# Silu tiles laid out group by group, and the stores of the first two gates moved to the end of pairs 4 and 5

## The chip, the core and the metric

The kernel runs on one core of one Trainium2 chip. The metric is the device time of one execution in microseconds (us). The kernel before took 1743.54 us (median of 3 runs, 1742.93 to 1745.15); the one execution that was profiled took 1740.37 us, of which the span from its first to its last instruction is 1738.6 us.

## What is computed

The input x has 4 images of 128 channels and 96 x 96 pixels. Each image is group-normalised and read as a sequence of 9216 steps in four orders (by rows and by columns, each forward and reversed). Each sequence goes through the same block:

```python
t = _grouped1x1(x, in_proj_w, in_proj_b, G)
u, gate = (t[:, :HID], t[:, HID:])
u = jax.nn.silu(u)
u = lax.conv_general_dilated(u, dw_w, ..., feature_group_count=HID)   # 5 taps per channel
s = _conv1x1(u, ssm_in_w)
a = DMIN + (DMAX - DMIN) * jax.nn.sigmoid(_conv1x1(u, ssm_delta_w, ssm_delta_b))
bb, cc = tanh of two more 1x1 products of u
hst = linear recurrence along the sequence: h = a * h + bb * s
u = u + _conv1x1(cc * hst + ssm_d[None, :, None] * s, ssm_out_w)
u = _grouped1x1(u * jax.nn.sigmoid(gate), mix_w, mix_b, G)
y = _conv1x1(u, out_proj_w, out_proj_b)
```

The four outputs are put back in image order, multiplied by the fuse matrix, summed, and added to x. All of it is float32; there are 256 hidden channels (`HID`) and 32 state channels (`MH`).

## The kernel before

**Tiling.** Two sequences that run in opposite directions are worked on side by side (index `s`). A sequence is cut into 6 strips of 16 lines (`NS`), a strip into 4 interleaved phases (`R`) of 384 columns (`N`). A *step* is one strip of the two sequences; a *pair* is one phase of a step for both of them, and the main loop runs over 192 pairs: `pair(t)` for t = 0 to 5, then `pair_on(t)`, which also finishes pair t - 6. Eight passes (4 images, two orientations) have 24 pairs each (`NP`).

**The silu tile.** `front` computes, 4 pairs ahead of their use, the silu of one of the 4 groups `g` of a step: TensorE multiplies `x_in` by the normalised input weights (L130, called from `in_proj_tile`) and ScalarE applies silu (L514) into `sils[step]`. That tile holds 2 sequences `s`, 2 halves of the channels `j`, 4 groups `g` and 385 columns, indexed `[:, s, j, g, :]`. It is read by the convolution's matmuls (`conv`, `conv_less`), by the taps on ScalarE and VectorE (`taps`, L729 and L731), and by DMAs.

**What is kept in DRAM.** The second half of a pass uses the silu of the first half's strips again, mirrored: the third and second strip's from SBUF, the first strip's from DRAM. So the silu of the first strip of each pass is stored group by group (`keep_silu`, L494) and loaded back for the last strip (`load_silu`, L500): 64 such DMAs in the kernel. Likewise the tanh of the gates of the first 12 pairs of a pass are stored to `kept` and loaded later. In the first pass the gate of pair n is worked out in two halves, in pairs 2n and 2n + 1 (L580), n = 0, 1, 2; gates 0 and 1 stay in the two SBUF tiles `gates[0]`, `gates[1]` until pairs 6 and 7 use them, gate 2 goes into a shared tile and is loaded back from DRAM at pair 6 (L599). The stores are issued at the end of pairs 1, 3 and 5 (L935). The silu stores of the first pass are issued at the end of pairs 0 and 1.

**Order of the work.** The order is written out by hand. Every DMA but one is issued by SyncE (SP), in program order. A DMA names one of eight semaphores in turn, so that one of them also waits until the DMA eight places ahead of it has landed. The work around the change is that of pairs 0 to 7. There, `pair(t)` does on TensorE: convolution of the pair, `front(t + 4)`, projections of the pair (`u,main` in the rows), the gate's product. The rows of `x_in` for the next step are loaded by `after_front` (L297): half of them one phase at a time, after each group, and the other half for all four phases at once after group 3, which for step 2 is in pair 3. Pair 4 computes `front(8)`, the first group of step 2, and needs those. `load_gate` (L315) loads rows for gates, `load_chunks` (L429) chunks of the next image for its statistics, `keep_lone` (L663) stores and `load_lone` (L669) loads two edge rows of a step's silu.

Of the kernel before, what the change touches and what calls it, by code (L numbers as in the profile page):

```python
# [42 lines left out]
F32 = mybir.dt.float32  # L43
# [4 lines left out]
P = 128  # L48
# [11 lines left out]
N = LN * WW // R  # L60
# [8 lines left out]
def conv_preact_kernel(  # L69
# [9 lines left out]
    nc = tc.nc  # L79
# [221 lines left out]
    def gate_at(un):  # L301
        return (un["p"] + PAD) % R, (un["p"] + PAD) // R

    def mirror(n):

        if n % NP < NP // 2:
            return None
        st, k = divmod(n % NP, R)
        return (NS - 1 - st) * R + TURN.index(R - 1 - TURN[k])

    def load_gate(i):
        if i < NU and mirror(i // 2) is None:
            un = units[i]
            q, _ = gate_at(un)
            nc.sync.dma_start(  # L315
                x_in[un["s"]][half(1 - un["s"]), q, :],
                xs[un["b"], un["lay"], half(1 - un["s"]), q, bass.ds(un["st"] * N, N + 1)],
            )
# [63 lines left out]
    for s in range(2):  # L382
# [18 lines left out]
    wk = ctx.enter_context(tc.tile_pool(name="work", bufs=2))  # L401

    gates = [wk.tile([P, 2, 2, N], F32, tag=f"gate{e}", bufs=1, name=f"gate{e}") for e in range(2)]
    kept = [
        [dp.tile([P, 2, 2, N], F32, tag=f"kept{e}_{m}", name=f"kept{e}_{m}") for m in range(NP // 2)]
        for e in range(2)
    ]
# [25 lines left out]
    def stats_chunks(t):  # L433
# [5 lines left out]

    sils = {}  # L440

    kept_sil = [
        [dp.tile([P, 2, 2, N + 1], F32, tag=f"sil{e}_{g}", name=f"sil{e}_{g}") for g in range(R)]
        for e in range(2)
# [6 lines left out]
    def front_parts(i, banks, half=False):  # L451

        step, g = divmod(i, R)
        if step * UB >= NU:
            return
        st = step % NS
        if st in (NS // 2, NS // 2 + 1):
            sils[step] = sils[step - 1 - 2 * (st - NS // 2)]
        elif st == NS - 1 and g < 3:
            load_silu(step, (g + 1,))  # L460
        elif g == 0 and fresh(step):
            sils[step] = wk.tile([P, 2, 2, 4, N + 1], F32, tag="sil", name=f"sil_{step}")
        if fresh(step):
            yield from compute_front(step, g, banks, half)
        if st == 0:
            for j in range(2):
                edges(step, g, j, nc.gpsimd)
        after_front(step, g)
# [26 lines left out]

    def load_silu(step, gs):
        if 0 in gs:
            sils[step] = wk.tile([P, 2, 2, 4, N + 1], F32, tag="sil", name=f"sil_{step}")
        for g in gs:
            nc.sync.dma_start(sils[step][:, :, :, g, :], kept_sil[step // NS % 2][g])  # L500

# [86 lines left out]
    def keep(n):  # L588
        return kept[n // NP % 2][n % NP]
# [3 lines left out]
    def tile_of(n):  # L593
        return gates[n % 2]
# [8 lines left out]
    def load_last(t):  # L603

        n = NU // 2 - R
        if t == n:
            lasts.append(wk.tile([P, 2, 2, 4, N + 1], F32, tag="sil", name="last_gates"))
        for e in ((0, 1), (), (2,), (3,))[t - n]:
            old_gates[n + e] = lasts[0][:, :, :, e, :N]
            nc.sync.dma_start(old_gates[n + e], kept[n // NP % 2][mirror(n + e)])  # L610

    lasts = []
# [285 lines left out]
    early = [None]  # L898

    def pair(t):  # L900
        i = 2 * t
        banks = head_banks(t)
        if t == R:
            load_lone(1)
        if t:
            new_u(i)
            taps(i, range(1, K))
            single = alone(units[i]["p"])
            conv(i, banks, single)
            if single:  # L910
                add_lone(i, banks)
            else:
                conv_less(i, banks, False)
                for s in range(2):
                    nc.vector.tensor_copy(us[i][:, s, 0, :], bank(min(banks) + s)[:, :N])
            first_tap(i + 2)
            front(t + R, FRONT if banks == PROJ else (5, 4, 2, 3))
        recurrence(t)
        stats_chunks(t)
        load_chunks(t + 2)  # L920
        proj(i, banks)
        n, s = divmod(t, 2)
        if s == 0:
            early[0] = tile_of(n) if n < 2 else shared()[:, : 4 * N].rearrange(
                "p (s j n) -> p s j n", s=2, j=2
            )
        for j in range(2):
            gate(2 * n, s, j, 2 + j)
        for j in range(2):
            tanh_one(n, early[0], s, j, 2 + j)  # L930
        load_gate(2 * n + s + UB)
        for g in {0: (0, 1), 1: (2, 3)}.get(t, ()):
            keep_silu(0, g)
        if s:
            nc.sync.dma_start(kept[0][n], early[0])  # L935
        if t > 0:
            s = tbs[i - 2][0:64, :]
            nc.gpsimd.tensor_scalar(s, s, d_sb[0:64, 0:1], None, ALU.mult)
# [232 lines left out]
    def start():  # L1171
        def filler(n):
            nc.tensor.matmul(
                bank(7)[:, :n], accf[:, bass.ds(10 * SC, P)], accf[:, bass.ds(10 * SC, n)],
                start=True, stop=True,
            )

        def outer(d, i, copy):
            for j in range(2):
                nc.tensor.matmul(  # L1180
                    bank(i)[:, bass.ts(j, P)], w_out[:, bass.ts(j, P)], w_fuse[:, d, :],
                    start=True, stop=True,
                )
            copy(w_of[:, d].rearrange("p j c -> p (j c)"), bank(i)[:, : 2 * P])

        def inner(ds, i):
            for n, (d, j) in enumerate((d, j) for d in ds for j in range(2)):
                nc.tensor.matmul(  # L1188
                    bank(i)[:, bass.ts(n, P)], w_mix[:, j, :], w_of[:, d, j, :],
                    start=n == 0, stop=True, skip_group_check=True,  # L1190
                )
            to = w_fin[:, ds[0] : ds[-1] + 1].rearrange("p d j c -> p (d j c)")
            nc.vector.tensor_scalar_mul(to, bank(i), 0.5)

        pieces = stats_first(b0)
        for n in (512, 512, 512):
            filler(n)
        next(pieces)
        for n in (512, 512):
            filler(n)  # L1200
        next(pieces)
        outer(0, 0, nc.scalar.copy)
        outer(1, 1, nc.scalar.copy)
        next(pieces)
        outer(2, 4, nc.scalar.copy)
        next(pieces)
        outer(3, 5, nc.vector.tensor_copy)
        filler(128)
        for _ in pieces:
            pass  # L1210
        sils[0] = wk.tile([P, 2, 2, 4, N + 1], F32, tag="sil", name="sil_0")
        banks = ((2, 3), (6, 7), (0, 1), (4, 5)), ((2, 3), (6, 7), (4, 5), (2, 3))

        def burst(j, g):
            for s in range(2):
                in_proj(0, g, s, j, banks[j][TURN.index(g) if j else g][s])

        def silus(j, g):
            for s in range(2):
                silu(0, g, s, j, banks[j][TURN.index(g) if j else g][s])  # L1220
            edges(0, g, j, nc.vector)

        def load_rows(j, r):
            for s in range(2):
                load_front(1, s, slice(64 * s + 32 * j, 64 * s + 32 * j + 32), r)

        for g in range(R):
            burst(0, g)
        silus(0, 0)
        burst(1, TURN[0])  # L1230
        silus(0, 1)
        burst(1, TURN[1])
        silus(0, 2)
        inner((0, 1), 0)
        inner((2, 3), 1)
        for w in (w_of, w_fuse):
            for e in (2, 1):
                nc.gpsimd.tensor_add(w[:, 0:e], w[:, 0:e], w[:, e : 2 * e])
        load_rows(0, slice(0, R))
        load_rows(1, slice(TURN[0], TURN[0] + 1))  # L1240
        silus(0, 3)
        new_u(0)
        burst(1, TURN[2])
        silus(1, TURN[0])
        taps(0, (0,), nc.vector)
        burst(1, TURN[3])
        load_rows(1, slice(TURN[1], R))
        load_rows(1, slice(0, TURN[0]))
        silus(1, TURN[1])
        taps(0, (1,))  # L1250
        conv(0, head_banks(0))
        silus(1, TURN[2])
        taps(0, (2,))
        silus(1, TURN[3])
        conv_less(0, head_banks(0))
        taps(0, (3, 4))
        keep_lone(0)
        load_lone(0)
        pf = bank(3)
        terms = [(w_of[:, 0, j, :], b_mix[:, j : j + 1]) for j in range(2)] + [(w_fuse[:, 0, :], b_out)]  # L1260
        for i, (lhsT, rhs) in enumerate(terms):
            nc.tensor.matmul(pf[:, 0:1], lhsT, rhs, start=(i == 0), stop=(i == len(terms) - 1))
        nc.scalar.activation(b_fin, pf[:, 0:1], AF.Identity, bias=b_fuse)
# [94 lines left out]
```

## Time and profile before

| | us |
|---|---|
| median of 3 runs | 1743.54 (1742.93 to 1745.15) |
| profiled execution, whole | 1740.37 |
| its span, first to last instruction | 1738.6 |
| TensorE busy | 1715.3 |
| VectorE busy | 1504.6 |
| ScalarE busy | 1494.7 |
| GpSimd busy | 1452.5 |
| DMA packets | 176,436 with 363.47 MB, a mean of 209 GB/s |

In the rows of the profile PE is TensorE's matmul, PEld its weight load, DVE VectorE, ACT ScalarE, POOL GpSimd and SPq the queue of SyncE that issues DMAs. L130 is line 130 of the kernel. A row of a timeline gives start, duration, engine, line, operation, `out<-in`, shape, a count, and in square brackets how long the engine was idle ahead of it and what ended that. A row that merges several instructions runs from the first one's start to the last one's end. A row of DMAs gives the size of one and the median time from issue to landing. The granted TensorE clock is 1.00 throughout.

### The profile page before, as it was taken

What the parts mean: (1) busy time and instruction counts of PE and PEld (TensorE: products, weight loads), DVE (VectorE), ACT (ScalarE), POOL (GpSimd) and SP (SyncE); (2) the same over time, 40 slices, a digit from 0 to 9 for tenths busy, and PEclk for the clock granted to TensorE, in tenths of its full rate; (3) what the DMA queues carried; (4) which work ended last, traced back from release to release, by engine and by line L of the source; (5) the groups of instructions that cost most, each with busy time, mean ns of one, the idle gap of its engine ahead of it and who ended that gap; (6) DMA issues with size and microseconds to landing.
All of it is one profiled execution on the core that took longest, in us unless ns stands there. A gap on an engine that the chain in (4) does not pass through costs nothing.

```text
span 1738.6 us, 54363 instructions
## 1 busy us (share of the span) xinstructions
PE 1715.3 (99%) x22626; PEld 644.7 (37%) x22626; DVE 1504.6 (87%) x1505; ACT 1494.7 (86%) x2544; POOL 1452.5 (84%) x1496
## 2 busy tenths in 40 slices
PE   7999999999999999999999999999999999999998
PEld 3233333333333433344333443334333343333333
DVE  6899998888889999888888999888888888888897
ACT  4788888889888898888988888888998888888875
POOL 3589889888779988988788988898878889887887
PEclk9999999999999999999999999999999999999999
DMA  7846965368984786337896488433897549743465
GB/s 239 229 157 202 300 194 151 116 214 271 283 280 151 249 272 200 116 124 255 257 309 226 151 298 258 145 120 133 290 287 249 179 140 294 213 135 135 148 224 167
DMA packets 176436, 363.47 MB, mean 209 GB/s; under 512 B 16704, under 2 KB 150848, under 8 KB 176192
## 3 DMA queue, kind: packets, MB, share of 16 engines
q1 hardware_dynamic: 176048, 359.96, 64.7%
q8 instruction: 179, 2.93, 0.7%
q14 instruction: 65, 0.53, 0.1%
q10 hardware_dynamic: 144, 0.04, 0.0%
HBM read 221.41 MB, written 138.53 MB: 207 GB/s over the span
## 4 chain that ended last, share of the span: by engine, by line
PE 95%; DMA 2%; DVE 1%; ACT 1%; issue 0%; SPq 0%; DVEq 0%
PE psum L130 81%; PE psum L564 8%; PE psum L544 5%; DMA x_in<-in_xs 1%; DVE psum L731 1%; DMA acc<-in_xr 0%; DVE u L625 0%; ACT psum L576 0%; DVE u L731 0%; ACT psum L729 0%; SPq L327 0%; PE psum L1188 0%; ACT sil L514 0%; ACT t L777 0%; ACT shared L580 0%
## 5 line engine op out<-in xcount | busy, mean ns | idle before, releaser
L731 DVE SCALAR_TENSOR_TENSOR psum<-sil,small,psum 128x768 f32<-128x768 f32 x576 | 589.1, 1023 | 42.1 <-ACT psum L729 16.6
L130 PE MATMUL psum<-u,w_fin 128*32 128x384 f32 (+1 forms) x6192 | 541.6, 484 | 1.1 <-ACT ys L847 0.5
L130 PE MATMUL psum<-u,main 128*32 128x384 f32 x6144 | 535.1, 489 | 0.5 <-DVE u L678 0.4
L625 DVE SCALAR_TENSOR_TENSOR u<-gate,psum 128x768 f32<-128x768 f32 x376 | 341.8, 950 | 154.7 <-PE psum L564 54.5
L866 POOL TENSOR_TENSOR acc<-ys,acc 128x384 f32<-128x384 f32 x375 | 422.7, 1149 | 13.9 <-ACT ys L847 1.9
L812 POOL TENSOR_TENSOR t<-t,t 64x384 f32<-64x384 f32 (+1 forms) x192 | 277.4, 1445 | 70.8 <-DVE t L806 53.6
L576 ACT COPY psum<-u 128x768 f32<-128x768 f32 x384 | 301.4, 799 | 10.5 <-DVE u L625 4.4
L130 PEld LDWEIGHTS psum<-u,w_fin 128*32 128x32 f32 x6192 | 195.9, 110 | 308.8 <-issue 235.7
L130 PEld LDWEIGHTS psum<-u,main 128*32 128x32 f32 x6144 | 180.0, 109 | 324.5 <-issue 217.4
L130 PE MATMUL psum<-sil,band 128*32 128x384 f32 x3072 | 285.3, 488 | 0.0
L779 POOL TENSOR_SCALAR t<-tm 64x384 f32<-64x384 f32 x184 | 172.5, 937 | 113.4 <-ACT tm L768 101.5
L813 POOL TENSOR_TENSOR t<-t,t 64x384 f32<-64x384 f32 (+1 forms) x192 | 233.9, 1218 | 15.1
L780 POOL TENSOR_TENSOR t<-t,tm 64x384 f32<-64x384 f32 x192 | 213.1, 1110 | 28.4 <-ACT t L771 13.6
L564 PE MATMUL psum<-t,main 32*128 32x384 f32 x1536 | 228.3, 525 | 4.2 <-ACT psum L576 4.2
L729 ACT ACTIVATE psum<-sil,small 128x768 f32<-128x768 f32 x191 | 172.4, 903 | 62.0 <-DVE u L625 60.1
L731 DVE SCALAR_TENSOR_TENSOR u<-sil,small,psum 128x768 f32<-128x768 f32 x192 | 194.9, 1015 | 6.8
L514 ACT ACTIVATE sil<-psum,bnorm 128x385 f32<-128x385 f32 x384 | 191.8, 584 | 7.4 <-PE psum L130 5.2
L544 PE MATMUL psum<-x_in,wn 32*128 32x384 f32 x768 | 161.6, 498 | 0.0
L849 ACT COPY ys<-psum 128x384 f32<-128x384 f32 x288 | 132.4, 478 | 32.9 <-PE psum L130 27.3
L130 PEld LDWEIGHTS psum<-sil,band 128*32 128x32 f32 x3072 | 88.9, 108 | 171.4 <-issue 63.3
L768 ACT ACTIVATE tm<-psum,small 128x384 f32<-128x384 f32 x192 | 110.8, 577 | 16.3 <-PE psum L130 6.2
L564 PEld LDWEIGHTS psum<-t,main 32*128 32x128 f32 x1536 | 94.0, 183 | 73.7 <-issue 42.9
(106 smaller groups left out, 1510.9 us busy)
## 6 DMA issues: line engine op xcount, KB each, us to landing
gate<-kept SPq DMA_DIRECT2D x114, 768.0 KB, 5.7
kept<-gate SPq DMA_DIRECT2D x74, 768.0 KB, 3.6
sil<-sil SPq DMA_DIRECT2D x64, 770.0 KB, 7.8
lone<-edge SPq DMA_DIRECT2D x40, 770.0 KB, 8.5
x_in<-in_xs SPq DMA_DIRECT2D x250, 96.2 KB, 3.3
edge<-sil SPq DMA_DIRECT2D x96, 192.5 KB, 3.9
out<-acc SPq DMA_DIRECT2D x46, 384.0 KB, 6.9
acc<-in_xr SPq DMA_DIRECT2D x39, 384.0 KB, 6.7
```

Of the source, the lines that this page charges most:

```text
L130: nc.tensor.matmul(o[r, : rhs.shape[-1]], lhsT, rhs, start=start, stop=stop, skip_group_check=True)
L514: nc.scalar.activation(sils[step][:, s, j, g, :], bank(bk)[:, : N + 1], AF.Silu, bias=bn[:, 1:2] if j else bn[:, 4 + g : 5 + g],)
L544: nc.tensor.matmul(bank(to)[:, :N], stats[un["b"]][0][r, s, :], x_in[s][r, q, off : off + N], start=True, stop=True)
L564: nc.tensor.matmul(bank(ssm(bi, s) + j)[:, :N], w_so[r, bass.ts(j, P)], z[r, :], start=(bi, s) not in seeded, stop=True, skip_group_check= ...
L576: nc.scalar.copy(psum[:, ssm(bi, s) : ssm(bi, s) + 2, :N], us[bi][:, s])
L625: nc.vector.scalar_tensor_tensor(v, g, 1.0, pz, ALU.add, ALU.mult)
L731: nc.vector.scalar_tensor_tensor(us[i][:, :, 1, :] if k == K - 1 else part, src, w_tap[:, k : k + 1], part, ALU.mult, ALU.add,)
L779: nc.gpsimd.tensor_scalar(*decay(i))
L780: nc.gpsimd.tensor_mul(ta[0:64, p, :], tb[0:64, :], tm[0:64, :])
L812: engine.tensor_mul(ta[0:64, p, r], tb[64:P, r], ta[64:P, p, r])
L813: engine.tensor_add(tb[0:64, r], ta[0:64, p, r], tb[0:64, r])
L866: adder.tensor_add(part, y, part)
```

## The change

The silu tile keeps its index order, but its memory within a partition is now ordered by group first: `[g, s, j, n]` in place of `[s, j, g, n]`. All four places that make such a tile call `new_sil`. What a partition stores or loads of one group was four runs of 1540 bytes that lay apart, and is one run of 6160 bytes. Gates 0 and 1 are stored at the end of pairs 4 and 5 from the gate tiles; gate 2 is still stored in pair 5, ahead of gate 1.

```diff
+    def new_sil(of):
+
+        t = wk.tile([P, 4, 2, 2, N + 1], F32, tag="sil", name=f"sil_{of}")
+        return t.rearrange("p g s j n -> p s j g n")
...
-            sils[step] = wk.tile([P, 2, 2, 4, N + 1], F32, tag="sil", name=f"sil_{step}")
+            sils[step] = new_sil(step)
...
-            lasts.append(wk.tile([P, 2, 2, 4, N + 1], F32, tag="sil", name="last_gates"))
+            lasts.append(new_sil("last"))
...
         load_gate(2 * n + s + UB)
+        if n == 2 and s:
+            nc.sync.dma_start(keep(n), early[0])
         for g in {0: (0, 1), 1: (2, 3)}.get(t, ()):
             keep_silu(0, g)
-        if s:
-            nc.sync.dma_start(kept[0][n], early[0])
+        if t > 3:
+            nc.sync.dma_start(keep(t - 4), tile_of(t - 4))
```

SyncE's queue from the second two silu stores (end of pair 1) to the stores of the edge rows (pair 4) was, before the change, this; `sil_2_204` and `sil_3_205` are DRAM copies of groups 2 and 3, `kept_0_178` is gate 0's, `x_in_70` and `x_in_71` are the two sequences' input tiles, and the two rows `32x4x385` are what `front(8)` of pair 4 needs:

```order
L494 DMA sil_2_204<-sil_291 512x1x385
L494 DMA sil_3_205<-sil_291 512x1x385
L935 DMA kept_0_178<-gate_176 128x1536
L297 DMA x_in_70<-in_xs 32x385
L297 DMA x_in_71<-in_xs 32x385
L429 DMA xs_0_607<-in_xr 128x384
L315 DMA x_in_70<-in_xs 64x385
L297 DMA x_in_70<-in_xs 32x4x385
L297 DMA x_in_71<-in_xs 32x4x385
L297 DMA x_in_70<-in_xs 32x385
L297 DMA x_in_71<-in_xs 32x385
L663 DMA edge_1_211<-sil_439 32x4x385 x4
```

The same stretch after the change:

```order
L499 DMA sil_2_204<-sil_291 128x1540
L499 DMA sil_3_205<-sil_291 128x1540
L297 DMA x_in_70<-in_xs 32x385
L297 DMA x_in_71<-in_xs 32x385
L429 DMA xs_0_606<-in_xr 128x384
L315 DMA x_in_70<-in_xs 64x385
L297 DMA x_in_70<-in_xs 32x4x385
L297 DMA x_in_71<-in_xs 32x4x385
L297 DMA x_in_70<-in_xs 32x385
L297 DMA x_in_71<-in_xs 32x385
L668 DMA edge_1_211<-sil_439 32x4x385 x4
```

The store of gate 0 has left this stretch, and the two silu stores have 128 pieces of 1540 elements where they had 512 of 385.

SyncE's queue from the end of pair 3 to pair 6, before; `xs_` are chunks of the next image:

```order
L315 DMA x_in_71<-in_xs 64x385
L935 DMA kept_1_179<-gate_177 128x1536
L669 DMA lone_715<-edge_1_211 128x4x385
L315 DMA x_in_70<-in_xs 64x385
L429 DMA xs_3_844<-in_xr 128x384
L315 DMA x_in_71<-in_xs 64x385
L935 DMA kept_2_180<-shared 128x1536
L429 DMA xs_4_915<-in_xr 128x384
L599 DMA gate_176<-kept_2_180 128x1536
```

And after:

```order
L315 DMA x_in_71<-in_xs 64x385
L674 DMA lone_713<-edge_1_211 128x4x385
L315 DMA x_in_70<-in_xs 64x385
L942 DMA kept_0_178<-gate_176 128x1536
L429 DMA xs_3_843<-in_xr 128x384
L315 DMA x_in_71<-in_xs 64x385
L938 DMA kept_2_180<-shared 128x1536
L942 DMA kept_1_179<-gate_177 128x1536
L429 DMA xs_4_915<-in_xr 128x384
L604 DMA gate_176<-kept_2_180 128x1536
```

Gate 1's store moved from ahead of the edge rows' load to behind gate 2's, and gate 0's now stands behind pair 4's `x_in` load. On TensorE, VectorE, ScalarE and GpSimd the instructions and their order are the same in both kernels; only the places in SBUF that they read and write of a silu tile differ.

More of the change, by code (lines that the diff above doesn't have):

```diff
@@ L497, in load_silu @@
         if 0 in gs:
-            sils[step] = wk.tile([P, 2, 2, 4, N + 1], F32, tag="sil", name=f"sil_{step}")
+            sils[step] = new_sil(step)
         for g in gs:
@@ L1210, in start @@
             pass
-        sils[0] = wk.tile([P, 2, 2, 4, N + 1], F32, tag="sil", name="sil_0")
+        sils[0] = new_sil(0)
         banks = ((2, 3), (6, 7), (0, 1), (4, 5)), ((2, 3), (6, 7), (4, 5), (2, 3))
```

## Prediction

> **What bounds the kernel.** I read the page first.
>
> ```profile
> PE 1715.3 (99%) x22626; PEld 644.7 (37%) x22626; DVE 1504.6 (87%) x1505; ACT 1494.7 (86%) x2544; POOL 1452.5 (84%) x1496
> PE 95%; DMA 2%; DVE 1%; ACT 1%; issue 0%; SPq 0%; DVEq 0%
> ```
>
> PE is busy for 99% of the span and makes 95% of the chain that ended last. A change to DMAs can gain only where PE stands still, so I next read PE's busy time by stretches (length first, then PE busy).
>
> ```profile
> 60.00:64.00 4.00, 2.38 (x48) 0.82 (x44) 3.68 (x4) 1.41 (x4) 0.41 (x1) 1.00 0.82 205
> ...
> 100.00:500.00 400.00, 399.98 (x5344) 149.91 (x5344) 352.98 (x348) 354.31 (x606) 345.29 (x357) 1.00 0.68 218
> ...
> 1500.00:1655.00 155.00, 154.99 (x2040) 57.64 (x2036) 132.52 (x124) 136.35 (x233) 129.85 (x122) 1.00 0.45 150
> ```
>
> From 100 to 1655 us PE idles for hundredths of a microsecond per stretch. Whatever the other 60 silu stores and loads gain there, PE does not wait for it: 0 us. The view of waits, for PE from 24 to 1655 us, names all that is left between the loading at the start and the tail.
>
> ```profile
> PE psum L130 <- DMA x_in<-in_xs: 1.9, 2, 1.6
> PE psum L564 <- ACT psum L576: 1.3, 1, 1.3
> PE psum L130 <- DVE u L678: 0.4, 2, 0.2
> ```
>
> One wait of 1.6 us is for a DMA, a load of `x_in`. PE's timeline around it shows pair 4 and, as a measure, pair 5, which does the same work without waiting.
>
> ```profile
> 59.29 0.88 PE L130 MATMUL psum<-sil,less 64*32 64x384 f32 x16
> 61.78 1.78 PE L130 MATMUL psum<-x_in,wn 32*32 32x385 f32 x32 [1.62 <-DMA x_in<-in_xs]
> 63.48 2.79 PE L130 MATMUL psum<-u,main 128*32 128x384 f32 x32
> ...
> 68.47 0.88 PE L130 MATMUL psum<-sil,less 64*32 64x384 f32 x16
> 69.28 1.04 PE L130 MATMUL psum<-x_in,wn 32*32 32x385 f32 x32
> 70.25 2.79 PE L130 MATMUL psum<-u,main 128*32 128x384 f32 x32
> ```
>
> From `less` to `u,main` pair 4 takes 63.48 - 59.29 = 4.19 us and pair 5 70.25 - 68.47 = 1.78. The late load costs **2.41 us**: the wait, and 0.74 us by which `x_in`'s matmuls last longer (1.78 for 1.04), since the second sequence's load comes later still. That is all that the change can take from PE here.
>
> **Why the load is late.** The chain of waits has the load; SyncE's timeline shows when it and the DMAs ahead of it were issued.
>
> ```profile
> 53.93 7.71 DMA x_in<-in_xs
> ```
>
> ```profile
> 46.06 0.60 SPq L494 DMA_DIRECT2D sil<-sil  x1
> ```
>
> ```profile
> 46.70 0.64 SPq L494 DMA_DIRECT2D sil<-sil  x1
> 47.44 1.32 SPq L935 DMA_DIRECT2D kept<-gate  x1
> ```
>
> ```profile
> 55.61 4.25 SPq L297 DMA_DIRECT2D x_in<-in_xs  x3
> ```
>
> These are the last two silu stores, gate 0's store, and the second of the two loads (first of three in its row). The DMA view, taken at each of these four issues, gives the time to landing:
>
> ```profile
> sil<-sil SPq DMA_DIRECT2D x1, 770.0 KB, 9.5
> ```
>
> ```profile
> sil<-sil SPq DMA_DIRECT2D x1, 770.0 KB, 11.2
> ```
>
> ```profile
> kept<-gate SPq DMA_DIRECT2D x1, 768.0 KB, 12.0
> ```
>
> ```profile
> x_in<-in_xs SPq DMA_DIRECT2D x1, 192.5 KB, 6.8
> ```
>
> The stores land at 46.06 + 9.5 = 55.6, 46.70 + 11.2 = 57.9 and 47.44 + 12.0 = 59.4 us, one behind the other, and the loads at 53.93 + 7.71 = 61.6 and 55.61 + 6.8 = 62.4. The DMA share (the figure before the last) shows a backlog:
>
> ```profile
> 40.00:62.00 22.00, 19.99 (x296) 6.59 (x300) 17.76 (x20) 17.24 (x32) 9.73 (x10) 1.00 1.02 269
> 62.00:72.00 10.00, 10.00 (x156) 3.29 (x144) 7.60 (x8) 7.28 (x14) 3.14 (x3) 1.00 0.94 281
> 72.00:84.00 12.00, 10.59 (x152) 3.19 (x147) 10.81 (x14) 9.72 (x18) 10.32 (x11) 1.00 0.39 134
> ```
>
> The engines are full from 40 to 62 us, so what is taken out ahead of the loads brings them forward by its whole service time.
>
> **The change, part by part.**
>
> *Gate 0's store leaves the stretch.* It landed 59.4 - 57.9 = 1.5 us behind the silu store ahead of it: the loads come 1.5 us earlier, to 60.1 and 60.9.
>
> *The four silu stores have 128 pieces for 512.* One took 57.9 - 55.6 = 2.3 us; gate 0's store, of the same size in long pieces, 1.5. So merging is worth between 0 and 0.8 us a store, and 0 to 3.2 for four. I take half, 1.6 us, since the gate's 1.5 us may hold some overlap with what went before. With it the loads would land at 58.5 and 59.3. [...]
>
> *The second load is issued sooner.* It went out at 55.61, as the silu store eight places ahead landed (55.6). With gate 0's store gone, the DMA eight places ahead is a small `x_in` load ahead of the silu stores in the queue, so it can follow the first at once.
>
> *When PE needs them.* Without the wait, `x_in`'s matmuls begin 69.28 - 68.47 = 0.81 us behind `less`: at 60.10, and the second sequence's half of 1.04 us later, at 60.6. Both loads are there (58.5, 59.3). Even with nothing from merging, the second would cost 0.3 us (60.9 - 60.6). So this wait gives back 2.1 to 2.4 us.
>
> *What is late next.* VectorE and ScalarE did not stand behind PE's wait in all they did.
>
> ```profile
> 66.27 1.01 DVE L731 SCALAR_TENSOR_TENSOR u<-sil,small,psum 128x768 f32<-128x768 f32 x1
> 69.51 1.02 DVE L915 COPY u<-psum 128x384 f32<-128x384 f32 x2 [2.23 <-PE psum L130]
> ```
>
> ```profile
> 68.38 0.91 ACT L729 ACTIVATE psum<-sil,small 128x768 f32<-128x768 f32 x1
> 70.20 2.00 ACT L514 ACTIVATE sil<-psum,bnorm 128x385 f32<-128x385 f32 x4 [0.91 <-PE psum L130]
> 72.51 0.58 ACT L768 ACTIVATE tm<-psum,small 128x384 f32<-128x384 f32 x1 [0.31 <-issue]
> ```
>
> VectorE's taps of pair 5 end at 67.28 whatever PE does. PE 2.41 us earlier would like the copy at 67.10: 0.2 us late. ScalarE's next tap overwrites what those taps read, so it runs from 67.3 to 68.2 (68.38 - 2.41 = 65.97 is not open to it); the silu behind it begins at 68.2 for 67.79 and ends at 70.2, and L768 begins there, 0.1 to 0.2 us behind its shifted time 70.10. From L768 on ScalarE is busy without a break to the wait of 1.3 us of pair 6 (the row of L576), so this delay is kept. I take **0.2 us** off: 2.41 - 0.2 = 2.2 us.
>
> *Gates 0 and 1 stored in pairs 4 and 5.* Both wait for nothing new, as their tiles are long written. They come to lie from 67 to 78 us, where the DMA share is 0.39 from 72. Behind gate 1's store on SyncE stands the chunk `xs_4`:
>
> ```profile
> 75.28 0.33 SPq L935 DMA_DIRECT2D kept<-shared  x1
> 79.22 0.33 SPq L429 DMA_DIRECT2D xs<-in_xr  x1
> ```
>
> ```profile
> xs<-in_xr SPq DMA_DIRECT2D x1, 192.0 KB, 3.0
> ```
>
> ```profile
> 86.84 1.02 DVE L437 BATCH_NORM_STATS2 bn<-xs 128x6 f32<-128x384 f32 x2
> ```
>
> Shifted by 2.2 us, gate 2's and gate 1's stores go out at 73.1 and 73.4 and, at 2.3 us each at most, are through by 78; `xs_4` goes out at 77.0 and lands by 81. VectorE wants it at 84.6: 3.6 us to spare, so 0 us. Without that cover VectorE, and PE behind it, would wait for what the stores exceed it by.
>
> *The layout on the compute engines.* Runs stay 384 or 385 words long; only offsets permute. 0 us.
>
> **Sum.** 2.2 us off the profiled execution's 1740.37 us gives 1738.2. That execution lies 3.2 us under the median of 1743.54 that the result will be held against, so the prediction is 1743.5 - 2.2 = **1741.3 us**.
>
> **Rivals.**
>
> 1. *The wait stays.* The loads might not follow the stores' order, or another queue's packets fill the gap; then the gain is 0 to 0.8 us: about 1743.1. Against it: five DMAs land in the order of their issue. Chance 0.10.
> 2. *The change doesn't do what it says:* the stores are still cut into 1540-byte pieces. Then gate 0's 1.5 us work alone: 2.1 - 0.2 = 1.9, 1741.6. Gate stores of one run are an example against it. Chance 0.05.
> 3. *More goes.* The 1.3 us of ScalarE and the 0.4 us of VectorE fall too: 2.2 + 1.7 = 3.9, 1739.6. Against it: both hang on work that PE itself releases. Chance 0.05.
> 4. *Slower: the matmuls that read silu slow down at their new offsets.*
>
> ```profile
> L130 PE MATMUL psum<-u,main 128*32 128x384 f32 x6144 | 535.1, 489 | 0.5 <-DVE u L678 0.4
> L130 PE MATMUL psum<-sil,band 128*32 128x384 f32 x3072 | 285.3, 488 | 0.0
> ```
>
> PE has no slack, so each per cent on 285.3 us is 2.9 us. It decides against the gain from 0.8% on; 3% gives 1743.5 + 8.6 - 2.2 = 1749.9. Against it: 488 ns from the silu tile and 489 from `u`, whose offsets differ, show no dependence. Chance 0.05.
>
> **How the numbers follow.** The forecast has 0.75: 1741.1 to 1741.6 by its bounds, and 1740.5 to 1743.2 with the scatter of the three runs (0.6 below their median, 1.6 above). The range reaches down to rival 3 and up past rival 1: 1739.5 to 1744.0. About 0.2%, 3.5 us, is what a measurement can tell from no change. All but rival 4 and the scatter's edge lie within it: same 0.86. Faster by more has 0.08 (rival 3 with scatter), slower 0.06 (rival 4).
>
> **What would show it.** Right: PE's `x_in` row of pair 4 without a wait and 1.04 us long, `u,main` near 61.1; silu stores near 1.5 us apart; the 1.3 us wait of L564 still there, at 76.6; the stretches from 100 us on unchanged. Wrong: PE waiting for `x_in` still, or for VectorE behind L437 near 84.6, or means of the silu matmuls above 488 ns.

## The result, and the profile after

The changed kernel takes 1738.72 us (median of 22 executions, 1737.42 to 1745.79). The kernel before, executed 22 times beside it, takes 1743.50 us (1738.73 to 1749.8). The ratio is 0.9974, with a 95% interval from 0.9965 to 0.9983: faster by 0.26%, 4.8 us where 2.2 were forecast. The time lies just under the range that was given.

The one execution of the changed kernel that was profiled is not one of the typical ones: it took 1742.29 us, with a span of 1740.3, and so was *longer* than the profiled execution of before (1740.37 and 1738.6). Its page, the lines on busy time, packets and the chain:

```profile
PE 1716.6 (99%) x22626; PEld 645.5 (37%) x22626; DVE 1509.3 (87%) x1505; ACT 1495.9 (86%) x2544; POOL 1451.3 (83%) x1496
...
DMA packets 151860, 363.47 MB, mean 209 GB/s; under 512 B 16704, under 2 KB 118080, under 8 KB 151616
...
PE 94%; DMA 2%; DVE 2%; ACT 1%; issue 0%; POOL 0%; SPq 0%; DVEq 0%; ACTq 0%; POOLq 0%
```

The bytes are the same and the packets 24,576 fewer: the merged runs. PE's waits in the same window as before, from 24 to 1655 us:

```profile
PE psum L569 <- ACT psum L581: 1.3, 1, 1.3
PE psum L130 <- DVE u L683: 0.4, 2, 0.2
PE psum L130 <- ACT shared L591: 0.3, 1, 0.3
PE psum L130 <- DMA x_in<-in_xs: 0.2, 1, 0.2
```

The 1.6 us for `x_in` in pair 4 are gone, and nothing of that size has come in their place. And yet the span is longer. The stretches of this execution show why (the figure behind the parentheses, third from the end, is the granted TensorE clock):

```profile
24.00:26.00 2.00, 1.81 (x51) 1.02 (x59) 0.12 (x2) 1.34 (x3) 0.00 (x0) 1.00 0.46 139
26.00:32.00 6.00, 6.00 (x68) 4.05 (x53) 0.66 (x5) 4.56 (x10) 0.32 (x1) 0.51 0.32 84
32.00:36.00 4.00, 4.00 (x60) 1.89 (x61) 2.79 (x7) 2.00 (x4) 2.84 (x4) 0.88 0.22 55
60.00:64.00 4.00, 4.00 (x56) 1.08 (x52) 2.88 (x3) 3.48 (x6) 2.85 (x3) 1.00 0.82 225
100.00:500.00 400.00, 399.98 (x5344) 149.56 (x5336) 354.07 (x347) 354.59 (x605) 345.28 (x358) 1.00 0.66 217
1500.00:1655.00 155.00, 154.99 (x2044) 57.64 (x2036) 133.75 (x126) 136.08 (x232) 129.47 (x124) 1.00 0.45 148
```

From 26.10 to 32.93 us, in the start, PE was granted half its clock. It is busy for all of 26 to 32 us there, but with 68 matmuls. In another profiled execution of the same kernel (run e9 below, span 1736.3 us) the clock stayed at 1.00, and the stretch held 104:

```profile
26.00:32.00 6.00, 6.00 (x104) 3.33 (x86) 3.06 (x10) 5.74 (x13) 3.11 (x4) 1.00 0.40 102
```

So the two profiled executions that came with the result can't be set against each other. e9's stands in for after in what follows, since it ran at the clock that before's profiled execution had. Its timeline of PE through pairs 4 to 6 answers to the rows of the prediction:

```profile
59.48 0.88 PE L130 MATMUL psum<-sil,less 64*32 64x384 f32 x16
60.28 1.12 PE L130 MATMUL psum<-x_in,wn 32*32 32x385 f32 x32
61.33 2.79 PE L130 MATMUL psum<-u,main 128*32 128x384 f32 x32
...
76.67 0.93 PE L569 MATMUL psum<-t,main 32*128 32x384 f32 x8 [1.27 <-ACT psum L581]
```

and the last of them stood in before's timeline as

```profile
78.85 0.93 PE L564 MATMUL psum<-t,main 32*128 32x384 f32 x8 [1.27 <-ACT psum L576]
```

From `less` to `u,main` pair 4 now takes 61.33 - 59.48 = 1.85 us for 4.19 us: 2.34 less. From `less` to the `t,main` matmuls that wait in pair 6 it is 17.19 us for 19.56: 2.37 less. The spans differ by 1738.6 - 1736.3 = 2.3. At an equal clock the change is worth what the wait cost, and hardly anything is given back.

The result is twice that. The question for the experiments was where the other 2.5 us come from.

### The profile page after: what moved, and what is told of

The parts are those of the page before. It is cut to its first block, busy times and chain, and to the rows that moved or that the text cites. A ratio compares the mean times of both kernels' runs of the same rounds, so it can differ in the third digit from the quotient of the medians.

```text
span 1740.3 us, 54363 instructions
## 1 busy us (share of the span) xinstructions
PE 1716.6 (99%) x22626; PEld 645.5 (37%) x22626; DVE 1509.3 (87%) x1505; ACT 1495.9 (86%) x2544; POOL 1451.3 (83%) x1496
## 4 chain that ended last, share of the span: by engine, by line
PE 94%; DMA 2%; DVE 2%; ACT 1%; issue 0%; POOL 0%; SPq 0%; DVEq 0%; ACTq 0%; POOLq 0%
PE psum L130 81%; PE psum L569 8%; PE psum L549 5%; DMA x_in<-in_xs 1%; DVE psum L736 1%; DMA kept<-shared 0%; DMA acc<-in_xr 0%; DVE u L630 0%; ACT psum L581 0%; DVE u L736 0%; ACT psum L734 0%; PE psum L1195 0%; ACT sil L519 0%; SPq L327 0%; DVE u L683 0%
## 5 line engine op out<-in xcount | busy, mean ns | idle before, releaser
L871 POOL TENSOR_TENSOR acc<-ys,acc 128x384 f32<-128x384 f32 x375 | 413.9, 1126 | 13.5 <-ACT ys L852 1.9
L817 POOL TENSOR_TENSOR t<-t,t 64x384 f32<-64x384 f32 (+1 forms) x192 | 286.0, 1490 | 72.0 <-DVE t L811 53.2
L818 POOL TENSOR_TENSOR t<-t,t 64x384 f32<-64x384 f32 (+1 forms) x192 | 234.5, 1221 | 15.1
L734 ACT ACTIVATE psum<-sil,small 128x768 f32<-128x768 f32 x191 | 172.5, 903 | 62.7 <-DVE u L630 59.4
L773 ACT ACTIVATE tm<-psum,small 128x384 f32<-128x384 f32 x192 | 111.1, 579 | 15.2 <-PE psum L130 4.4
```

The lines of the kernel that those rows point to most:

```text
L734: nc.scalar.activation(part, src, AF.Copy, scale=w_tap[:, 0:1])
L817: engine.tensor_mul(ta[0:64, p, r], tb[64:P, r], ta[64:P, p, r])
L818: engine.tensor_add(tb[0:64, r], ta[0:64, p, r], tb[0:64, r])
L871: adder.tensor_add(part, y, part)
```

## The experiments

Each run is timed in rounds beside the kernel before; ratios are to it, with 95% intervals. Four answers were on trial. **The forecast's** (A in the expectations): 2.2 us, and the rest is the draw of 22 executions. **The steady theory** (B in the expectations): every execution gains about 4.8 us, through something that the two profiles don't show. **The chance theory** (C): stretches at half clock fall on either kernel alike, and the first comparison caught few of them in after. **The clock theory** (D, which took shape on the way): the wait in pair 4 itself makes PE lose half its clock for a while in some executions of before, and this goes with the wait. A later one (E) is that the order of the start's work causes the stretch near 26 us.

**e1_before, e2_after and e9_after_again: both kernels again, unchanged**

> The kernel before, unchanged, for the granted clock of each of its executions. The profile after shows a stretch of 6.8 us at half the TensorE clock near 26 us, and its other executions with clock 1.000 have spans of 1735.5 to 1737.7 us. Theory A (the change gives 2.2 us by the wait at pair 4; the rest of the 4.8 us between the medians is how many executions have such stretches, which hits this kernel more often): executions with clock 1.000 have spans of 1738 to 1739 us, those with one stretch 1742 to 1743, and more than half of them have at least one. Theory B (the extra gain is steady, in every execution): clock 1.000 in most, and spans near 1741.

> The changed kernel, beside the one before on the same chip. Theory A: against executions of the kernel before with clock 1.000, its own with clock 1.000 are 2.0 to 2.4 us shorter, spans 1736 to 1737. Theory B: 4 to 5 us shorter at equal clock. Theory C (the clock's slow stretches have nothing to do with the change): as many executions with a clock below 0.9995 as in the kernel before, and a ratio of the medians of 0.9987.

> The changed kernel once more, to see which of 0.9974 (the result) and 0.999 (the first run beside the kernel before) is the rule. At clock 1.000 the kernels lie 2.1 us apart (1738.6 and 1740.7); the wait at pair 4 adds 1.9 us in the third of the executions of the kernel before that show 0.999: 2.1 + 0.6 = 2.7 us on average, a ratio of 0.9984. Theory C/D (stretches of half clock at the start fall on both kernels by chance): ratio 0.9975 to 0.9995, clock 1.000 at 1738.0 to 1739.5. Theory B (a steady 4.8 us): ratio 0.9973 and clock 1.000 at 1736.

Before against itself measured 1741.52 us, ratio 1.0001 (0.9992 to 1.001). After measured 1740.37 against 1741.83, ratio 0.999 (0.998 to 1.0), and the second time 1738.24 against 1742.97, ratio 0.9978 (0.9969 to 0.9988). The same two kernels thus gave 4.8, 1.5 and 4.7 us. e2's profiled execution again had the half clock in the start, from 25.98 to 32.8 us. A kernel whose difference to another comes out between 1.5 and 4.8 us doesn't have one time but a few, and the mean granted clock that is recorded for each execution sorts them. All executions beside the experiments, and those of after:

| kernel | executions | clock 1.000: count, median us | 0.999 | 0.998 and under |
|---|---|---|---|---|
| before | 103 | 45, 1740.64 | 32, 1742.85 | 26, 1744.91 |
| after (result, e2, e9) | 46 | 27, 1738.33 | 5, 1738.14 | 14, 1742.18 |

A stretch of 3.41 us at half clock takes a mean over 1738 us to 0.999, and one of 6.83 us to 0.998. At 1.000 the kernels lie 2.3 us apart (95% by resampling: 1.8 to 2.7), far from 4.8: the steady theory falls. At 0.998 and under, the share is 14 of 46 against 26 of 103, 30% and 25%: the stretch in the start comes to both, and no effect of the change on it is to be seen. What differs is the middle: 31% of before's executions are at 0.999 and cost 2.2 us more, 11% of after's are and cost nothing. As far as these counts show, theory C holds for the start and not for the middle.

**e3_layout_only and e4_moved_only: each part of the change alone**

e3 is after with the gate stores where they were, and e4 is before with the gate stores moved:

```diff
 e3, against after:
-        if n == 2 and s:
-            nc.sync.dma_start(keep(n), early[0])
...
-        if t > 3:
-            nc.sync.dma_start(keep(t - 4), tile_of(t - 4))
+        if s:
+            nc.sync.dma_start(kept[0][n], early[0])
 e4, against before: the same lines the other way round
```

> The silu layout alone, gates 0 and 1 stored in pairs 1 and 3 as before. In the profile after, the silu stores land 1.4 to 1.5 us apart for 2.3 to 2.5 before, so four of them take 3.4 us less; with gate 0's 1.5 us still there the loads for pair 4 should land near 58.2 and 59 us, ahead of the 60.1 and 60.6 at which TensorE wants them. Theory A: wait of pair 4 gone, 2.0 to 2.3 us shorter than the kernel before at equal clock. Rival (the gate's store alone is what holds the loads up): 0 to 0.5 us shorter.

> The stores of gates 0 and 1 moved to pairs 4 and 5, the silu layout as before. The loads lose the 1.5 us of gate 0's store ahead of them: landing near 60.1 and 60.9. Theory A: a wait of 0.0 to 0.4 us stays at pair 4, 1.8 to 2.2 us shorter than the kernel before at equal clock. Rival (the many short pieces are what holds the loads up): 0 to 1 us shorter.

e3 measured 1738.64 us, ratio 0.9986 (0.9975 to 0.9997), and e4 1738.62, ratio 0.9982 (0.9974 to 0.9991). Either part alone does what both do together. PE's waits, of e3:

```profile
PE psum L569 <- ACT psum L581: 1.3, 1, 1.3
PE psum L130 <- DVE u L683: 0.4, 2, 0.2
```

and of e4:

```profile
PE psum L130 <- DVE u L678: 0.4, 2, 0.2
PE psum L130 <- DMA x_in<-in_xs: 0.2, 1, 0.2
PE psum L564 <- ACT psum L576: 0.2, 1, 0.2
```

The wait of pair 4 is gone from both. Of their 23 executions 2 are at 0.999 and 2 under; the others lie at 1738.54 and 1738.68 us (medians at 1.000), as after does. With after, the kernels without the wait have 7 of 69 at 0.999 and 16 of 69 under it (23%, before: 25%). The costly middle group goes with the wait.

e4's profiled execution is one of its rare ones at 0.999, and shows how a stretch can cost nothing (none of after's at 0.999 was profiled):

```profile
70.80:74.20 3.40, 3.25 (x44) 0.94 (x44) 3.29 (x5) 3.33 (x8) 3.17 (x4) 1.00 0.39 123
74.20:77.60 3.40, 3.23 (x24) 0.98 (x16) 1.71 (x3) 2.89 (x5) 3.25 (x4) 0.50 1.03 417
```

The half clock falls on 74.2 to 77.6 us, ahead of pair 6's wait for ScalarE. PE comes later, and that wait shrinks from 1.27 to the 0.2 us of the list above. Here a slower PE in front of a wait was free.

**e6_before_long_wait: a longer wait in pair 4**

Before, with two more stores of the gate's size behind gate 0's, so that `x_in` lands later still:

```diff
         if s:
             nc.sync.dma_start(kept[0][n], early[0])
+        if t == 1:
+            for e in range(2):
+                spare = dp.tile([P, 2, 2, N], F32, tag=f"spare{e}", name=f"spare{e}")
+                nc.sync.dma_start(spare, early[0])
```

> The kernel before, with gate 0's store made three times (twice more into DRAM that nobody reads), so that the loads for pair 4 land 3.0 to 3.8 us later and TensorE waits 4.5 to 5 us there. Theory D: a stretch of half clock follows the wait in nearly every execution, no execution at 1.000, and the time is 1740.7 + 3 to 3.8 + 1.7 to 3.4 = 1745.5 to 1748. Theory C: clocks spread as in the kernel before, at 1.000 a time of 1743.7 to 1744.5. If the queue behind gate 0's store were not what the loads wait for: 1740.7.

It measured 1745.59 us, ratio 1.0024 (1.0013 to 1.0034). The wait is 3.59 us, where 4.5 to 5 were expected; but of 11 executions none is left at clock 1.000 (45 of 103 in before; exact test 0.003): 2 are at 0.999 and 9 under. The stretches of the profiled one, and its PE timeline:

```profile
57.00:60.00 3.00, 3.00 (x44) 0.90 (x36) 2.31 (x3) 2.94 (x6) 2.42 (x3) 1.00 1.02 417
60.00:64.40 4.40, 0.81 (x27) 0.21 (x16) 3.80 (x4) 0.38 (x1) 0.72 (x1) 1.00 0.85 266
64.40:67.80 3.40, 3.40 (x44) 0.85 (x32) 3.06 (x3) 2.11 (x4) 0.00 (x0) 0.51 0.96 210
67.80:72.00 4.20, 4.20 (x46) 1.21 (x38) 0.00 (x0) 2.67 (x6) 1.99 (x3) 0.99 0.98 317
```

```profile
64.04 2.24 PE L130 MATMUL psum<-x_in,wn 32*32 32x385 f32 x32 [3.59 <-DMA x_in<-in_xs]
66.20 3.59 PE L130 MATMUL psum<-u,main 128*32 128x384 f32 x32
```

PE stands still for most of 60 to 64.4 us. From 64.45 to 67.87 us, 3.41 us right behind the wait, its clock is halved: `u,main` takes 3.59 us for 2.79. So the half clock follows a long wait in pair 4 here, and no execution with the long wait kept its clock throughout.

**e5_before_filled and e10_filled_again: the wait filled with work**

Before, with one full-width matmul (128 rows, 512 columns, its result not used) ahead of pair 4's `x_in` matmuls, in the time in which PE waits anyway. The wait's length stays; only its idleness goes. By the clock theory the middle group should go, though the load is as late as ever.

```diff
+            if t == R:
+                for n in (512,):
+                    nc.tensor.matmul(bank(5)[:, :n], accf[:, bass.ds(10 * SC, P)],
+                                     accf[:, bass.ds(10 * SC, n)], start=True, stop=True)
             front(t + R, ...)
```

> The kernel before, with one matmul of 128x512 (1.25 us, a product nobody reads) on TensorE ahead of pair 4's x_in matmuls, where TensorE waits 1.1 to 1.6 us. The wait's length stays; TensorE is kept working in it. So far 13 of 47 executions of the kernel before have clock 0.999 and a median 1.9 us above those with 1.000; in the kernels without the wait 6 of 57, at no cost. Theory D (the wait with the x_in matmuls around it makes the clock halve for one stretch of 3.4 us in a quarter of the executions): executions with 0.999 at 1742 to 1743 us all but vanish (0 or 1 of 12), those with 1.000 stay at 1740.5 to 1741. Theory C (chance, not the wait): 3 of 12 as before.

> The kernel before with the matmul of 1.25 us in pair 4's wait once more, for the count: theory D says 0 or 1 of 11 or 12 executions with clock 0.999 (26 of 80 in the kernel before, 0 of 11 in this one so far), theory C 3 or 4. Executions with 1.000 at 1740 to 1741.5.

PE's timeline in e5:

```profile
59.91 0.88 PE L130 MATMUL psum<-sil,less 64*32 64x384 f32 x16
60.71 1.12 PE L919 MATMUL psum<-acc 128*128 128x512 f32 x2
61.86 1.74 PE L130 MATMUL psum<-x_in,wn 32*32 32x385 f32 x32
63.53 2.79 PE L130 MATMUL psum<-u,main 128*32 128x384 f32 x32
```

The filler takes 1.12 us, and `x_in`'s matmuls begin as late as in before (61.86 against 61.78). The times: 1743.42 us, ratio 0.9998 (0.9986 to 1.001), and 1741.32, ratio 0.9999 (0.9986 to 1.0012). The middle group is all but gone: 1 of 23 executions at 0.999 for 32 of 103. That 32 in 103 give 1 in 23 or a count as uneven by chance has a probability of 0.008 (exact test). 13 are at 1.000 with a median of 1740.83 us, as before's, since the load is no earlier.

But the time didn't come down with it: the ratios are 1, and the mean of the 23 is 1742.6 us against 1742.4 for before. 9 of 23 are at 0.998 and under (39% for 25%; the exact test gives 0.2), which eats what the middle group gave. So the filler speaks for the idleness of pair 4 as what makes the group at 0.999; that removing the group alone shortens the mean is not shown. The difference of the two means is only known to about 1.1 us either way (95% by resampling), which is more than the group could give.

**e8_long_wait_filled: the long wait, filled**

e6 with three such matmuls in the wait, `(512, 512, 512)` in place of `(512,)`.

> As the kernel with the three stores, with three matmuls of 128x512 (3.75 us) on TensorE in the wait. Theory D: no half clock behind pair 4, most executions at 1.000, time 1743.7 to 1744.7, that is 1.7 to 3.4 us under the kernel with the three stores at equal wait. Theory C: the same time as that one.

It measured 1744.93 us, ratio 1.0018 (1.0009 to 1.0028): a little over the 1743.7 to 1744.7 expected, and 0.7 us under e6 where 1.7 to 3.4 were. Of its 11 executions 4 are at 1.000, not most; e6 has none. By an exact test such counts differ by chance with 0.09, so they decide little by themselves. The profiled one:

```profile
63.26 2.84 PE L919 MATMUL psum<-acc 128*128 128x512 f32 x6
66.91 1.77 PE L130 MATMUL psum<-x_in,wn 32*32 32x385 f32 x32 [0.81 <-DMA x_in<-in_xs]
```

```profile
66.00:69.50 3.50, 2.68 (x45) 0.81 (x48) 3.36 (x5) 1.67 (x4) 0.00 (x0) 1.00 0.78 192
```

The fillers leave 0.81 us of the wait, and no half clock follows it; the one of this execution lies in the start (25.12 to 31.94 us).

**e7_after_start_order: the start in another order**

After, with a product of full 128x128 matmuls (`inner`, L1195 in the rows) moved in between the first groups' small `x_in` matmuls, and the last two of those groups swapped, to break up the run of small matmuls ahead of 26 us:

```diff
-        for g in range(R):
+        for g in (0, 1):
+            burst(0, g)
+        inner((0, 1), 0)
+        for g in (3, 2):
             burst(0, g)
...
-        inner((0, 1), 0)
```

> The changed kernel, with the first of the two products of mix and fuse weights (full 128x128 matmuls, 1 us) moved between the second and third burst of x_in matmuls at the start, where it breaks a stretch of small matmuls from about 22.5 to 27.3 us; same instructions. In the profiles of the changed kernel the clock halves at 26.0 and 26.1 us for 6.8 us, and 12 of 34 executions have 0.998 or less, 3.4 us or more above the others. Theory E (that stretch of small 32-row matmuls is what halves the clock): at most 1 or 2 of 12 with 0.998 or less, those at 1.000 unchanged at 1738.0 to 1739.0. Theory C: 4 of 12 as before.

It measured 1740.46 us, ratio 0.9987 (0.9978 to 0.9997), so no better than after. 1 of 11 executions is at 0.998 or under, as theory E has it (at most 1 or 2), though against after's 14 of 46 that can be chance (0.26). But 4 are at 0.999, which cost here (1740.96 against 1739.41 at 1.000), and those at 1.000 are slower than the 1738.0 to 1739.0 expected. The half clock still comes at 26 us in the profiled execution, for 3.41 us and not 6.83:

```profile
22.60:26.00 3.40, 3.25 (x78) 1.63 (x78) 0.59 (x3) 2.63 (x7) 0.00 (x0) 1.00 0.60 151
26.00:29.40 3.40, 3.40 (x55) 1.77 (x54) 0.87 (x5) 0.41 (x1) 2.24 (x3) 0.50 0.01 2
```

The order of the start may set how long the stretch is; this one doesn't remove it. Theory E holds in part at best.

## Why the prediction was right or wrong

**The bound, and where the change can act: right.** From 100 us on the stretches are as before, PE idle for 0.02 us of 400 us. The silu's matmuls kept their mean, so rival 4 didn't come (e9, groups by form):

```profile
L130 PE MATMUL psum<-sil,band 128*32 128x384 f32 x3072 | 285.3, 488 | 0.0
```

**The late load's 2.41 us: right for that execution.** 2.34 us of it went, to `u,main` at 61.33 where "near 61.1" was foretold. `x_in`'s matmuls take 1.12 us, near pair 5's 1.04.

**The landing of the loads: right in kind, and merging worth more.** The DMA view at the issues of e9's last two silu stores (46.21 and 46.84 us) and of the two loads (54.12 and 54.82):

```profile
sil<-sil SPq DMA_DIRECT2D x1, 770.0 KB, 7.3
```

```profile
sil<-sil SPq DMA_DIRECT2D x1, 770.0 KB, 7.8
```

```profile
x_in<-in_xs SPq DMA_DIRECT2D x1, 192.5 KB, 3.7
```

```profile
x_in<-in_xs SPq DMA_DIRECT2D x1, 192.5 KB, 5.0
```

The stores land at 53.5 and 54.6 us, 1.1 us apart, where the unmerged ones were 2.3 apart: in this pair 1.2 us a store, three times the 0.4 that the sum took and over its bound of 0.8. The loads land at 57.8 and 59.8 us (58.5 and 59.3 foretold), ahead of PE's need at 60.28. That merging alone takes the whole wait away (e3) speaks plainly against 0 us, the lower end of the range that was given for it. The low estimate cost the sum nothing, as either part alone brings the loads in early enough.

**What is late next: right in kind, and worth nothing.** ScalarE does wait for VectorE's taps, and L773 begins when the silu ends, as foretold (e9):

```profile
67.50 0.91 ACT L734 ACTIVATE psum<-sil,small 128x768 f32<-128x768 f32 x1 [1.17 <-DVE u L736]
68.35 1.98 ACT L519 ACTIVATE sil<-psum,bnorm 128x385 f32<-128x385 f32 x4
70.33 0.58 ACT L773 ACTIVATE tm<-psum,small 128x384 f32<-128x384 f32 x1
```

But L773 moved from 72.51 to 70.33, by 2.18 us, and `u,main` by 2.15: ScalarE kept up with PE, and the 0.2 us were not lost. The wait of 1.3 us in pair 6 stayed, at 76.67 (76.6 foretold), so rival 3 didn't come.

**The moved gate stores: right.** `xs_4` went out at 77.04 us (77.0 foretold) and landed at 80.3, ahead of VectorE's need:

```profile
84.67 1.01 DVE L437 BATCH_NORM_STATS2 bn<-xs 128x6 f32<-128x384 f32 x2
```

**The sum: wrong in its last step**, "That execution lies 3.2 us under the median of 1743.54 that the result will be held against, so the prediction is 1743.5 - 2.2 = 1741.3 us." The sum against the profiled execution, 1738.2 us, is what after's executions at the same clock take (1738.33). The step then added 3.2 us back, as if the distance between that execution and the median were scatter that the change leaves alone. It isn't: before's profiled execution ran at clock 1.000, and so do only 44% of before's executions (45 of 103). The sum lacked a term: it has none for what the wait does to the clock, which was 1.00 throughout in the one profiled execution that it went by. The wait of pair 4 costs time in every execution, 2.41 us in that one and, in e1's profiled execution, also at clock 1.000, (63.13 - 59.57) - (69.93 - 68.12) = 1.75:

```profile
59.57 0.88 PE L130 MATMUL psum<-sil,less 64*32 64x384 f32 x16
61.58 1.62 PE L130 MATMUL psum<-x_in,wn 32*32 32x385 f32 x32 [1.14 <-DMA x_in<-in_xs]
63.13 2.79 PE L130 MATMUL psum<-u,main 128*32 128x384 f32 x32
...
68.12 0.88 PE L130 MATMUL psum<-sil,less 64*32 64x384 f32 x16
69.93 2.79 PE L130 MATMUL psum<-u,main 128*32 128x384 f32 x32
```

In 31% of the executions a stretch at half clock comes on top, 2.2 us by the medians (1742.85 - 1740.64). That is 0.31 x 2.2 = 0.7 us in the mean: 2.3 + 0.7 = 3.0 us. The means of before and of the three kernels without the wait (after, e3, e4) differ by 1742.4 - 1739.5 = 2.9.

The median makes more of it, since the times have several humps. With 44% at 1.000, before's median falls above that hump; with 59% at 1.000 and 11% at a harmless 0.999, after's falls inside. Over all executions of the table it goes from 1742.44 to 1738.76 us, by 3.7 us, which lies within the interval of the first result (3.0 to 6.1 us by its ratios).

**What stays open.** Of the first result's 4.8 us the last 1.1 are put down to its draw only by argument: the clocks of before's 22 executions there aren't recorded. No execution of before with 0.999 was profiled, so the place of its stretch, behind pair 4, is inferred from the counts of e3 to e6, e8 and e10. And the clock alone can take at most 1.7 us in 3.41 us, where the group at 0.999 costs 2.2. A longer wait in just those executions would explain the rest: the wait differs from one execution to the next (1.62 and 1.14 us), and with the 3.59 us of e6 no execution kept its clock. No run measured the wait in an execution at 0.999.

## What to carry to other kernels

Before a sum is set against a median, look at the granted clock of the profiled execution and of the others: here the profile at clock 1.000 showed the wait's own cost, 2.41 us, and not the half clock that, by the counts, came with it in other executions (31% at 0.999, 2.2 us longer by the medians). Removing this wait of 1.62 us was worth 2.9 us in the mean. Where the times have several humps, say which one the forecast is for. Where several DMAs land one behind the other, as here at 55.6, 57.9 and 59.4 us, any of those ahead of the late one that is shortened or moved may be enough, so a change in two parts should be tried part by part.

## What was not expected of the hardware

That a wait of 1.1 to 1.6 us, by the counts, goes with a halved clock: 32 of 103 executions of before are at 0.999, 7 of 69 without the wait and 1 of 23 with the filler. In before's profiled execution, which kept its clock, the stretch around the wait has PE busy for more than half the time:

```profile
59.30:63.50 4.20, 2.58 (x55) 0.72 (x51) 3.18 (x4) 1.61 (x3) 1.11 (x1) 1.00 0.80 185
```

and still 31% of its executions have the mean clock that one stretch of 3.41 us at half clock gives. More than that: in e4 from 70.8 to 74.2 us and in e7 from 22.6 to 26.0 us, PE was busy for 3.25 of 3.40 us, and half clock followed (0.50 in both). In e4 it ran there almost only matmuls with 32 rows (the gates and `x_in`):

```profile
70.83 0.92 PE L544 MATMUL psum<-x_in,wn 32*128 32x384 f32 x4
71.67 2.34 PE L130 MATMUL psum<-x_in,wn 32*32 32x385 f32 x32
```

But e9 ran the same work at the same place, and its mean clock is 1.000:

```profile
70.78 0.92 PE L549 MATMUL psum<-x_in,wn 32*128 32x384 f32 x4
71.63 2.35 PE L130 MATMUL psum<-x_in,wn 32*32 32x385 f32 x32
```

In the start it is alike. In after PE was busy for 3.81 of the 4.00 us from 22 to 26 (2.00 and 1.81), and the 6.83 us at half clock from 26.10 followed; in e9, the same kernel, it was busy there for 3.75 us, and the clock stayed at 1.00:

```profile
22.00:26.00 4.00, 3.75 (x115) 2.18 (x117) 1.13 (x8) 3.13 (x7) 0.00 (x0) 1.00 0.65 154
```

So in these executions neither PE's busy time ahead of a stretch nor the work itself tells which of them loses its clock. What decides it is not shown. No run varied the rows or columns of the matmuls by themselves.
